# Relaid pools, spread block ends and projection columns in a five-stage graph network kernel

## The chip, the cores and the metric

The kernel runs on one core of one Trainium2 chip. The metric is device time in microseconds (us), lower is better. The profiles are hardware profiles of single executions. All executions here are of the fast state as far as one core can tell, save one of the kernel before (3599.67 us, left out of its round's ratios). They still scatter by up to ±30 us; what goes with that is shown near the end.

## The reference, cut to what matters

2708 nodes with 512 features, a dense 0/1 adjacency matrix (about 2.4% ones), and four residual layers, each followed by a layer norm:

```python
# layer 0: mean over the first 64 neighbours of each row
keep = Ab & (cumsum(Ab, axis=1) <= 64)
xj = leaky_relu((keep @ X / max(cnt, 1)) @ W_nb.T + b_nb)
x = layernorm(x + leaky_relu(X @ W_line.T + b_line) + where(cnt > 0, xj, 0))
# layer 1: mean over all neighbours
nb = (mask @ x / deg) @ W_nb + b_nb
x = layernorm(x + relu(concat([x @ W_self + b_self, nb]) @ W_comb + b_comb))
# layers 2 and 3: graph attention with 8 heads of 64; s = Wh @ a1, d = Wh @ a2
e = leaky_relu(s[:, :, None] + d[:, None, :], 0.2)
h = softmax(where(adj > 0, e, -9e15)) @ Wh
# layer 3 goes on: elu, one more attention with a single head of 512 ("last"),
# elu, relu(@ lin1) @ lin2; then x = layernorm(x + h)
```

The kernel folds `W_self @ W_comb[:512]` and `W_nb @ W_comb[512:]` into one weight each. In what follows a "tile" is 128 nodes, so 22 tiles, the last of 20 rows.

## The kernel before

Layer 0's first stage makes `y = x @ W_nb.T` and the `W_line` term for each tile, and turns each row block of the adjacency matrix into a transposed mask. After it comes the folding of layer 1's weights, then layer 0's aggregation in blocks of four tiles:

```python
for t in range(NT):                                   # mask projection
    xt = fetched(sm, x, t, n, "xt")                   # two buffers
    xT = transposed(sm, ps_tr, xt, n, "xT")           # TensorE, copied out by ScalarE
    # pm = xT @ wnT -> keep_y ; pm = xT @ wlT -> u    (8 float32 matmuls)
    nc.gpsimd.tensor_add(u[:n], u[:n], xt)
    nc.scalar.dma_start(r0_dram[...], u[:n])
    mask(t)                                           # 22 transposes into PSUM
# ... here the weights of layer 1 are folded, TensorE, 58 us ...
for b0 in range(0, NT, 4):                            # aggregation
    kT = kept(0)                                      # cum on TensorE, compare on VectorE
    for j in range(NT):
        if j + 1 < NT:
            nxt = kept(j + 1)
        # pa[t] += kT.T @ yH[j], yL[j]  for the four tiles of the block
        kT = nxt
    for t in ts_:                                     # the block's end, all at once
        # bias, leaky, residual, layer norm on VectorE, store x1
```

The projections of layers 2, 3 and last (`project`) take s and d on VectorE and write v for all tiles at the end:

```python
for t in range(NT):
    xT = transposed(sm, ps_tr, source(sm, t, n), n, "xT")   # three row buffers
    # pm = xT @ w
    for i, col in enumerate((scol, dcol)):
        pr = sm.tile([P, D], F32, name="pr")
        nc.vector.tensor_mul(pr[:n], pm[:n], ab[:n, i, :])
        nc.vector.tensor_reduce(col[:n, t, :heads], pr..., AX.X, OP.add)
    # ecol, ucol = exp(d) ; R2 = pm * ecol ; vrow = exp(clipped s), transposed
nc.sync.dma_start(v_dram, vrow)          # attention reads it back, broadcast
# bcol and the parts (bfloat16 splits of ucol * ecol and ecol) for all tiles
```

Every stage opens its own pools for SBUF and PSUM, and each waits for the memory of one before it.

Of the kernel before, what the change touches and what calls it, by code (L numbers as in the profile page):

```python
# [29 lines left out]
def kernel(  # L30
# [34 lines left out]

    upper = const.tile([P, P], BF16, name="upper")
    make_upper_triangular(nc, upper)
    below = const.tile([P, P], BF16, name="below")
    nc.vector.tensor_scalar(below, upper, -1.0, 1.0, op0=OP.mult, op1=OP.add)
# [13 lines left out]
    scol = const.tile([P, NT, H], F32, name="scol")  # L83
    dcol = const.tile([P, NT, H], F32, name="dcol")
    for c in (scol, dcol):
        nc.vector.memset(c, 0.0)
# [6 lines left out]
    x1_dram = dram.tile([N, D], F32, name="x1_dram")  # L93
    z1_dram = dram.tile([N, D], F32, name="z1_dram")
# [23 lines left out]
    def transpose_weight(pool, psum, dst, src, queue):  # L118

        for ki in range(KD):  # L120
            wr = pool.tile([P, D], F32, name="wr", bufs=3)
            queue.dma_start(wr, src[ki * P:(ki + 1) * P, :])
            ps = psum.tile([P, KD, P], F32, name="ps_tr")
            for ko in range(KD):
                nc.tensor.transpose(ps[:, ko, :], wr[:, ko * P:(ko + 1) * P], ident)
            nc.vector.tensor_copy(dst[:, :, ki * P:(ki + 1) * P], ps)

    def fetched(pool, src, t, n, name, bufs=None):
        x_ = pool.tile([P, D], F32, name=name, bufs=bufs)
        nc.sync.dma_start(x_[:n], src[t * P:t * P + n, :])  # L130
        return x_[:n]

# [6 lines left out]

    with ExitStack() as phase:  # L140
        yp = phase.enter_context(tc.tile_pool(name="y", bufs=1))
        yH = yp.tile([P, NT, D], F32R, name="yH")
# [3 lines left out]
        b_nb = yp.tile([P, D], F32, name="b_nb")  # L146
        nc.scalar.dma_start(b_nb, bcast(l0_b_nb, D))
# [4 lines left out]

        with ExitStack() as ph:
            wp = ph.enter_context(tc.tile_pool(name="l0w", bufs=1))
            sm = ph.enter_context(tc.tile_pool(name="l0s", bufs=2))
            ps_tr = ph.enter_context(tc.tile_pool(name="ps_tr", bufs=2, space=PSUM))
            ps_mm = ph.enter_context(tc.tile_pool(name="ps_mm", bufs=2, space=PSUM))
            ps_tb = ph.enter_context(tc.tile_pool(name="ps_tb", bufs=2, space=PSUM))
            b_line = wp.tile([P, D], F32, name="b_line")
            nc.scalar.dma_start(b_line, bcast(l0_b_line, D))  # L160
            wnT = wp.tile([P, KD, D], F32, name="wnT")
            wlT = wp.tile([P, KD, D], F32, name="wlT")
            transpose_weight(sm, ps_tr, wnT, l0_w_nb, nc.sync)
            transpose_weight(sm, ps_tr, wlT, l0_w_line, nc.scalar)

            def mask(t):
                n = rows(t)
                m = sm.tile([P, N], BF16, name="m")
# [12 lines left out]
                for g0 in range(0, NT, G):  # L181
                    g1 = min(g0 + G, NT)
                    ps = ps_tb.tile([P, G, P], BF16, name="ps_tb")
# [8 lines left out]

            for t in range(NT):
                n = rows(t)
                xt = fetched(sm, x, t, n, "xt")
                xT = transposed(sm, ps_tr, xt, n, "xT")
                pm = ps_mm.tile([P, D], F32, name="pm")
                for k in range(KD):
                    nc.tensor.matmul(pm[:n], xT[:, k, :n], wnT[:, k, :], start=(k == 0), stop=(k == KD - 1))
                keep_y(t, n, pm)  # L200
                pm = ps_mm.tile([P, D], F32, name="pm")
                for k in range(KD):
                    nc.tensor.matmul(pm[:n], xT[:, k, :n], wlT[:, k, :], start=(k == 0), stop=(k == KD - 1))
# [4 lines left out]
                nc.scalar.dma_start(r0_dram[t * P:t * P + n, :], u[:n])  # L208
                mask(t)



        wp = phase.enter_context(tc.tile_pool(name="l1wp", bufs=1))
        wself = wp.tile([P, KD, D], F32, name="wself")
        wnb = wp.tile([P, KD, D], F32, name="wnb")
        bias1 = wp.tile([P, D], F32, name="bias1")
        with ExitStack() as ph:
            lw = ph.enter_context(tc.tile_pool(name="l1w", bufs=1))
            ps_tr = ph.enter_context(tc.tile_pool(name="ps_trw", bufs=2, space=PSUM))
            ps_mm = ph.enter_context(tc.tile_pool(name="ps_mmw", bufs=2, space=PSUM))  # L220
            ps_b = ph.enter_context(tc.tile_pool(name="ps_bw", bufs=1, space=PSUM))
            bcomb = lw.tile([P, D], F32, name="bcomb")
            nc.scalar.dma_start(bcomb, bcast(l1_b_comb, D))
            pb = ps_b.tile([P, D], F32, name="pb")
            for i, (w_in, b_in, dst) in enumerate(((l1_w_self, l1_b_self, wself), (l1_w_nb, l1_b_nb, wnb))):
                wT = lw.tile([P, KD, D], F32, name="wT")
                transpose_weight(lw, ps_tr, wT, w_in, nc.sync)
                wc = lw.tile([P, KD, D], F32, name="wc")
                nc.scalar.dma_start(wc, l1_w_comb[i * D:(i + 1) * D, :].rearrange("(k p) c -> p k c", p=P))
                bcol = lw.tile([P, KD], F32, name="bcol", bufs=2)  # L230
                with nc.allow_non_contiguous_dma(reason="512 numbers, once"):
                    nc.scalar.dma_start(bcol, b_in.rearrange("(k p) -> p k", p=P))
                for m in range(KD):
                    pm = ps_mm.tile([P, D], F32, name="pm")
                    for k in range(KD):
                        nc.tensor.matmul(pm, wT[:, k, m * P:(m + 1) * P], wc[:, k, :],  # L236
                                         start=(k == 0), stop=(k == KD - 1))
                    nc.scalar.copy(dst[:, m, :], pm)
                brep = lw.tile([P, KD, P], F32, name="brep")
                nc.vector.tensor_copy(brep, bcol[:, :, None].to_broadcast([P, KD, P]))  # L240
                for k in range(KD):
                    nc.tensor.matmul(pb, brep[:, k, :], wc[:, k, :],
                                     start=(i == 0 and k == 0), stop=(i == 1 and k == KD - 1))
            nc.vector.tensor_add(bias1, pb, bcomb)



        with ExitStack() as ph:
            sm = ph.enter_context(tc.tile_pool(name="l0b", bufs=2))
            ps_a = ph.enter_context(tc.tile_pool(name="ps_a0", bufs=1, space=PSUM))  # L250
            ps_c = ph.enter_context(tc.tile_pool(name="ps_c0", bufs=2, space=PSUM))
            for b0 in range(0, NT, 4):
                b1 = min(b0 + 4, NT)
                ts_ = range(b0, b1)
                cols, w = slice(b0 * P, b1 * P), (b1 - b0) * P
                r0 = {t: fetched(sm, r0_dram, t, rows(t), f"r0{t - b0}", 1) for t in ts_}
                cum = ps_c.tile([P, 512], F32, name="cum")
                pa = {t: ps_a.tile([P, D], F32, name=f"pa{t - b0}") for t in ts_}

                def kept(j):  # L260
                    nc.tensor.matmul(cum[:, :w], upper, maskT[:, j, cols], start=(j == 0), stop=True,  # L261
                                     skip_group_check=True)
                    kT = sm.tile([P, 512], F32R, name="kT", bufs=3)
                    nc.vector.scalar_tensor_tensor(kT[:, :w], cum[:, :w], KEEP, maskT[:, j, cols],  # L264
                                                   op0=OP.is_le, op1=OP.mult)
                    return kT

                kT = kept(0)
                for j in range(NT):
                    if j + 1 < NT:  # L270
                        nc.tensor.matmul(cum[:, :w], below, maskT[:, j, cols], start=False, stop=True,
                                         skip_group_check=True)
                        nxt = kept(j + 1)
                    for t in ts_:
                        for y in (yH, yL):
                            nc.tensor.matmul(pa[t], kT[:, (t - b0) * P:(t - b0 + 1) * P], y[:, j, :],  # L276
                                             start=(j == 0 and y is yH), stop=(j == NT - 1 and y is yL))
                    kT = nxt
                us = {}
                for t in ts_:  # L280
                    n = rows(t)
                    us[t] = sm.tile([P, D], F32, name=f"u{t - b0}", bufs=1)
                    nc.vector.scalar_tensor_tensor(us[t][:n], pa[t][:n], rkeep[:n, t:t + 1], b_nb[:n],
                                                   op0=OP.mult, op1=OP.add)
                for t in ts_:
                    n, u = rows(t), us[t]
                    leaky(u[:n], u[:n])
                    nc.vector.scalar_tensor_tensor(u[:n], u[:n], has[:n, t:t + 1], r0[t], op0=OP.mult, op1=OP.add)
# [698 lines left out]
```

## Time and profile before

| | before |
|---|---|
| median, the three runs known when the prediction was made | 3582.98 us (3557.87 to 3584.34) |
| span of the profiled run | 3581.7 us |
| TensorE (PE) busy | 3330.2 us, 93% |
| mean granted clock of TensorE | 0.944 |

Names of tiles that the profile lines use: kT is a kept mask, pa (before) or acc (after) the sums of layers 0 and 1, pm the product of a tile of rows with a weight (in the changed kernel's aggregation also the running count of neighbours, cum before), xT those rows transposed, po and pn the sums of the head attentions and of the last one, e the masked attention weights before the softmax's division. A wait row reads: engine, tile and line that waited, what ended the wait, then us in total, times, longest.

Only TensorE is close to full. The prediction below shows the lines that say so: its busy tenths over 40 slices, the busy time by stage, and its waits. In a row of busy time by stage the columns are the stretch and its length, then the busy us (and number of instructions) of PE, PEld (weight loads), DVE (VectorE), ACT (ScalarE) and POOL (GpSimd), then the granted clock of TensorE, the DMA share and GB/s.

### The profile page before, as it was taken

To read this page: it belongs to the slowest core of one execution; us is meant where nothing else is said; L and a number is where in the kernel's file an instruction comes from. 1 tells how busy PE (TensorE), PEld (TensorE's weight loads), DVE (VectorE), ACT (ScalarE), POOL (GpSimd) and SP (SyncE) were. 2 spreads that over 40 slices of the span, in tenths; PEclk is the share of its full clock that TensorE was granted. 3 is DMA by queue.
4 is the path that set the end of the run, shared out by engine and by line. 5 is a ranking of instruction groups with operands and counts; after the bars stand their busy time and mean duration, and the time that the engine had idled before them with its cause. 6 is when DMAs were issued, how large, how long until landed. Compare 5 with 4: busy or idle time off the path is not lost.

```text
span 3581.7 us, 39258 instructions
## 1 busy us (share of the span) xinstructions
PE 3330.2 (93%) x15914; PEld 1695.5 (47%) x15914; DVE 2001.2 (56%) x2526; ACT 1380.9 (39%) x1519; POOL 158.3 (4%) x188
## 2 busy tenths in 40 slices
PE   7989898899988999999977999999988999999998
PEld 4445565447863444443432444443443545454546
DVE  5542445212337888999868988989783222122122
ACT  2420000112222877888823878878740101010000
POOL 1210000000000000000021000000000000000000
PEclk9999899999999999999988999999899999999999
DMA  5540101212221000000052000000021000000000
GB/s 119 124 111 27 47 24 39 65 59 76 79 80 61 17 30 28 24 23 23 16 151 86 25 25 25 24 23 31 19 77 65 15 12 27 1 24 0 24 7 19
DMA packets 103809, 157.14 MB, mean 44 GB/s; under 512 B 22442, under 2 KB 44234, under 8 KB 103602
## 3 DMA queue, kind: packets, MB, share of 16 engines
q1 hardware_dynamic: 72236, 102.17, 9.2%
q10 hardware_dynamic: 25590, 37.71, 3.0%
q0 software_dynamic: 5792, 14.67, 2.5%
q8 instruction: 127, 2.08, 0.2%
q14 instruction: 64, 0.52, 0.0%
HBM read 124.62 MB, written 44.55 MB: 47 GB/s over the span
## 4 chain that ended last, share of the span: by engine, by line
PE 84%; DVE 6%; DMA 5%; issue 3%; POOL 1%; ACT 1%; SPq 0%; POOLq 0%; ACTq 0%; DVEq 0%
PE po L506 26%; PE pn L659 14%; PE pd L492 7%; PE pa L323 6%; PE pa L276 6%; PE pm L396 5%; PE pl L625 5%; PE pl L635 4%; PE pm L302 2%; PE pm L306 2%; DMA m<-in_adj_dram 2%; PE ps_t L524 1%; DMA o<-o_dram 1%; DVE m L171 1%; PE pm L236 1%
## 5 line engine op out<-in xcount | busy, mean ns | idle before, releaser
L453 DVE SCALAR_TENSOR_TENSOR e<-v_bc,ucol,maskT 128x1408 f32<-128x1408 f32 (+5 forms) x836 | 1191.1, 1477 | 447.6 <-PE pn L659 370.9
L461 ACT ACTIVATE c<-e,bcol 128x1300 bf16<-128x1300 f32 (+1 forms) x704 | 998.7, 1424 | 217.2 <-DVE e L453 174.8
L506 PE MATMUL po<-e,R 128*64 128x512 f32 (+4 forms) x4224 | 960.1, 566 | 14.7 <-issue 14.4
L506 PEld LDWEIGHTS po<-e,R 128*64 128x64 f32 (+1 forms) x4224 | 364.0, 140 | 515.5 <-issue 439.0
L659 PE MATMUL pn<-e,R 128*128 128x512 f32 (+3 forms) x1056 | 425.2, 544 | 8.2 <-DVE e L453 8.2
L659 PEld LDWEIGHTS pn<-e,R 128*128 128x128 f32 (+1 forms) x1056 | 190.9, 190 | 219.7 <-issue 219.5
L570 ACT ACTIVATE elu_e<-elu_e 128x512 f32<-128x512 f32 (+2 forms) x46 | 27.5, 603 | 632.5 <-DVE elu_e L569 631.8
L396 PE MATMUL pm<-w,xT 128*128 128x512 f32 (+1 forms) x528 | 247.6, 613 | 19.3 <-ACT xT L115 12.2
L115 ACT COPY xT<-ps_tr 128x512 f32<-128x512 f32 x110 | 60.1, 568 | 449.8 <-DMA x<-x_dram 344.5
L492 PE MATMUL pd<-c,parts_c 128*6 128x512 bf16 (+4 forms) x2112 | 221.4, 360 | 0.0
L492 PE MATMUL pd<-maskT,parts_m 128*6 128x512 fp8e4 (+2 forms) x2112 | 210.8, 361 | 9.8 <-DVE parts_m L371 9.8
L276 PE MATMUL pa<-yH,kT 128*128 128x512 f32 x484 | 216.7, 448 | 0.0
L625 PE MATMUL pl<-lin 128*128 128x256 f32 (+1 forms) x704 | 163.7, 394 | 38.2 <-DVE lin L572 38.2
L276 PE MATMUL pa<-yL,kT 128*128 128x512 f32 x484 | 193.9, 401 | 0.0
L323 PE MATMUL pa<-yH,mf 128*128 128x512 f32 x484 | 189.4, 391 | 3.6 <-ACT mf L320 3.6
L323 PE MATMUL pa<-yL,mf 128*128 128x512 f32 x484 | 189.2, 391 | 0.0
L264 DVE SCALAR_TENSOR_TENSOR kT<-cum,maskT 128x512 fp32r<-128x512 f32 (+1 forms) x132 | 84.8, 646 | 164.5 <-PE cum L261 164.5
L625 PEld LDWEIGHTS pl<-lin 128*128 128x128 f32 x704 | 137.5, 204 | 72.4 <-DVE lin L572 49.8
L396 PEld LDWEIGHTS pm<-w,xT 128*128 128x128 f32 (+1 forms) x528 | 94.9, 191 | 134.8 <-issue 102.0
L635 PE MATMUL pl<-lin,gT 128*128 128x512 f32 (+1 forms) x352 | 153.0, 592 | 0.0
L638 DVE TENSOR_TENSOR y<-pl,x 128x512 f32<-128x512 f32 (+1 forms) x22 | 15.2, 691 | 244.3 <-PE pl L635 244.3
L659 PE MATMUL pn<-e,ecol 128*128 128x512 f32 (+2 forms) x264 | 125.9, 559 | 0.0
(162 smaller groups left out, 2906.2 us busy)
## 6 DMA issues: line engine op xcount, KB each, us to landing
x<-x_dram SPq DMA_DIRECT2D x105, 256.0 KB
m<-in_adj_dram POOLq DMA_DIRECT2D x21, 677.0 KB, 6.7
v_bc<-v_dram SPq DMA_DIRECT2D x16, 704.0 KB
x_dram<-u ACTq DMA_DIRECT2D x42, 256.0 KB
o<-o_dram SPq DMA_DIRECT2D x42, 256.0 KB
v_bc<-v_dram SPq DMA_DIRECT2D x16, 650.0 KB
o_dram<-o SPq DMA_DIRECT2D x32, 256.0 KB
xt<-in_x_dram SPq DMA_DIRECT2D x21, 256.0 KB
```

The lines of the kernel that those rows point to most:

```text
L264: nc.vector.scalar_tensor_tensor(kT[:, :w], cum[:, :w], KEEP, maskT[:, j, cols], op0=OP.is_le, op1=OP.mult)
L276: nc.tensor.matmul(pa[t], kT[:, (t - b0) * P:(t - b0 + 1) * P], y[:, j, :], start=(j == 0 and y is yH), stop=(j == NT - 1 and y is yL))
L302: nc.tensor.matmul(pm[:n], xT[:, k, :n], wnb[:, k, :], start=(k == 0), stop=(k == KD - 1))
L323: nc.tensor.matmul(pa, mf[:, j - g0, :], y[:, j, :], start=(j == 0 and y is yH), stop=(j == NT - 1 and y is yL))
L396: nc.tensor.matmul(pm[:n], xT[:, k, :n], w[:, k, :], start=(k == 0), stop=(k == KD - 1))
L453: nc.vector.scalar_tensor_tensor(e[:n, :w], v[:n, :w], ucol[:n, j, h:h + 1], maskT[:n, j, c0:c0 + w], op0=OP.max, op1=OP.mult)
L461: nc.scalar.activation(c[:n, :w], e[:n, :w], AF.Sigmoid, bias=bcol[:n, j, h:h + 1], scale=STEP)
L492: nc.tensor.matmul(pd[i][g:g + 6, :c1 - c0], lhsT, rhs, start=(j < 2 and what == 0), stop=(j >= NT - 2 and what == 1))
L506: nc.tensor.matmul(po[i][HO * k:HO * k + HO, :c1 - c0], R2[:n, j, h * HO:(h + 1) * HO], e[:n, c0:c1], start=(j == 0), stop=(j == NT - 1))
L625: nc.tensor.matmul(pl[:, :w], self.lin1[:, k, f * P:(f + 1) * P], h[:, k, :w], start=(k == 0), stop=(k == KD - 1))
L635: nc.tensor.matmul(pl[:n], gT[:, f, (t - t0) * P:(t - t0) * P + n], self.lin2[:, f, :], start=(f == 0), stop=(f == KF - 1))
L659: nc.tensor.matmul(pn[:, k, :w], lhsT, e[:n, :w], start=(j == 0), stop=(j == NT - 1))
```

## The change

Its intent is to remove TensorE's pauses at stage borders and block ends, by five means:

1. The fold of layer 1's weights stands first; its result goes to memory and is loaded back later.
2. Layer 0's block ends are a generator (`finish`), stepped once per step of the next block; the next block's first kT is made in the last step of this one.
3. Rows of all stages share one pool of two buffers (`ahead`), weights another, so that loads can go out before a stage begins. Several stores move to SyncE's queue.
4. `wa` = weights times the attention vectors, summed per head, is made once during the mask projection (24 loads, products and sums); s and d then come from four narrow matmuls per tile (`psd`).
5. v, the parts and bcol are written per block of tiles rather than after the last tile.

```diff
+    with ExitStack() as ph:                      # part 1: the fold, first
+        ... nc.scalar.dma_start(w_dram[i][m * P:(m + 1) * P, :], wm)
@@ mask projection
+            def vectors():                       # part 4
+                for layer, (w_src, w_view, a_srcs, heads) in enumerate(atts):
+                    for i in range(2):
+                        ab = st.tile([P, D], F32, name="ab", bufs=1)
+                        nc.scalar.dma_start(ab.rearrange(...), a_srcs[i])
+                        for k in range(KD):
+                            wr = st.tile([P, D], F32, name="wr")
+                            nc.scalar.dma_start(*w_view(wr, w_src, k))
+                            nc.vector.tensor_mul(wr, wr, ab)
+                            nc.vector.tensor_reduce(wa[:, layer, k, i, :heads], ..., AX.X, OP.add)
+                            yield
-                xt = fetched(sm, x, t, n, "xt")
+                xt = fetched(x, t, n)            # part 3: the shared pool
...
+                if t >= 5:
+                    for _ in range(2):
+                        next(todo, None)
@@ aggregation
+                    elif i + 1 < len(cuts):      # part 2
+                        cum, nxt = begin(cuts[i + 1])
...
+                    next(todo, None)             # one step of the last block's end
...
+                todo = finish(ts_, us)
@@ project
+                psd = ps_v.tile([P, 2, H], F32, name="psd")
+                for k in range(KD):              # part 4
+                    nc.tensor.matmul(psd[:n, :, :heads], xT[:, k, :n], wa[:, layer, k, :, :heads], ...)
-                for i, col in enumerate((scol, dcol)):
-                    ... tensor_mul, tensor_reduce
...
+                if t == z - 1:                   # part 5: last tile of a block
+                    nc.sync.dma_start(v_dram[:, cols], vrow[:, ...])
+                    ... parts of this block
```

## The prediction

> **What bounds the kernel now.** I read the page first, then the busy time by stage, then PE's waits, then the order of time around each stage border. The page: PE is busy 93% of 3581.7 us, and the chain that ended last runs on it.
>
> ```profile
> PE 84%; DVE 6%; DMA 5%; issue 3%; POOL 1%; ACT 1%; SPq 0%; POOLq 0%; ACTq 0%; DVEq 0%
> PE   7989898899988999999977999999988999999998
> PEclk9999899999999999999988999999899999999999
> ```
>
> So only two things can save time: less work for PE, or fewer of its 251.5 us of idleness (3581.7 - 3330.2) together with the slow clock that follows each pause. The eights and sevens of the second and third line mark the stage borders. The windows by stage say where the idleness lies (columns: stretch, its us, then PE, PEld, DVE, ACT and POOL busy, the granted clock, the DMA share, GB/s):
>
> ```profile
> 0.00:246.00 246.00, 213.31 (x956) 110.31 (x956) 136.63 (x303) 82.76 (x133) 50.17 (x56) 0.98 0.53 116
> 246.00:304.50 58.50, 44.91 (x112) 21.66 (x113) 6.21 (x10) 4.68 (x8) 0.00 (x0) 0.80 0.25 77
> 304.50:634.00 329.50, 287.16 (x1227) 201.88 (x1225) 150.70 (x275) 0.00 (x0) 13.19 (x20) 0.93 0.10 33
> 1044.00:1153.50 109.50, 92.64 (x290) 43.81 (x294) 75.61 (x147) 26.24 (x110) 0.00 (x0) 0.94 0.22 62
> 1818.00:1946.00 128.00, 99.00 (x286) 42.32 (x286) 100.23 (x223) 26.35 (x109) 32.86 (x36) 0.93 0.39 114
> ```
>
> These are, in order: layer 0's projection with the mask; the folding of layer 1's weights; layer 0's aggregation; the projections of layers 2 and 3. The two head attentions (664.5 and 654 us, PE busy 97 and 98%) and the last one (875.7 us) keep their inner loops, so I leave them as they are. What PE waited for, all stages, its costliest rows (us in total, times, longest):
>
> ```profile
> PE cum L271 <- DVE kT L264: 41.2, 7, 8.8
> PE pl L625 <- DVE lin L572: 38.2, 6, 7.2
> PE ps_tr L113 <- DMA x<-x_dram: 22.2, 2, 11.6
> PE po L506 <- issue: 14.4, 2, 7.3
> PE ps_v L415 <- DVE b L411: 12.7, 8, 3.0
> ```
>
> The first row is layer 0's block ends: DVE finishes four tiles there while PE waits for the next kept mask. The second row (the last layer's block ends) is not touched by the change. The third and fourth are borders: a stage's first rows arrive late, and attention waits for the whole v to go to memory and back.
>
> A pause costs more than itself. In order of time, at a block end of layer 0 and a few us later:
>
> ```profile
> 366.69 0.58 PE L271 MATMUL cum<-maskT,below 128*128 128x512 fp8e4 x1 [7.81 <-DVE kT L264]
> 368.35 0.63 PE L276 MATMUL pa<-yH,kT 128*128 128x512 f32 x1
> ...
> 373.03 0.39 PE L276 MATMUL pa<-yH,kT 128*128 128x512 f32 x1
> ```
>
> After the 7.81 us wait the same matmul takes 0.63 instead of 0.39 us, and matmuls start 0.43 instead of 0.23 us apart, for some 4.5 us: about 2 us more are lost.
>
> **What the Trainium skill says.** "TensorE: Matmul & The Clock Gate", Part 1: PE falls to half its clock after about 3.4 us of idleness, and needs about 3.4 us of work to return. This trace agrees (0.43 against 0.23 us, for 4.5 us). The same page, "LDWEIGHTS": a load takes its columns divided by 1.2 GHz, 107 ns for 128. The trace agrees as a rate: eight loads in 0.97 us, one of them 0.19 long, so 0.11 us apart:
>
> ```profile
> 1797.28 0.97 PEld L524 LDWEIGHTS ps_t<-pick,dT 102*128 102x128 f32 x8
> ```
>
> "DMA: Bandwidth & Descriptors", "Why small descriptors are slow", gives 27% overhead at 256 bytes; here the head weights come in 256-byte pieces, and beside them the first x of layer 2 landed after 5.7 us (issued 1044.78, PE at 1050.5), against 2.9 at layer 1's start (642.34 to 645.2). "TensorE: Matmul & The Clock Gate", the table at its head: the other engines are strict FIFO, so a DVE or ACT instruction that waits holds all behind it; the 7.81 us above agree.
>
> **The change part by part.** The scheduler places instructions by readiness (the loads of layer 3's rows stand ahead of the last stores of layer 2 in the trace, 1797 against 1803), so I assume that loads with a free buffer really go ahead.
>
> 1. *Fold first, then the projection.* Now the first product is at 25.6 us, the projection runs to 246, the fold to 304.5, the first pa at 306.9. The 64 + 16 fold matmuls at 0.43 are 34.4 us; with transposes, 12 us for the first 1 MB and the cold start I take 58. Then eight transposed weight tiles at 0.75 us: 6. All rows and the first two masks are there by then. The projection now takes 22 tiles in 221 us, 10.0 each, of which PE needs 16 x 0.43 + 22 mask transposes at 0.06 + 0.66, about 9. The chain there is a loop of POOL's add, 5.3 us of issue, 6.7 of mask DMA, 3.0 of DVE's count and 2.4 more of DVE, for two tiles. Four PSUM buffers for the mask help a little. Against it, the vectors for the s and d columns put 24 x (0.68 + 0.68) = 33 us on DVE, 6 MB on the DMA rings and up to 1 us per issue on ACT, over twelve tiles; some hides in DVE's idle 109 us of 246. I take 10.2 per tile, 225. Sum 58 + 6 + 225 = 289: **-17**. This is my weakest term (-40 to +5).
> 2. *Layer 0's block ends spread.* A steady step is 2.30 us, in the last block 1.16: 22 x (5 x 2.30 + 1.16) = 278.5, against 329.5: 51 to gain. The spread work is 3.8 us of DVE per tile, 76 in all, beside 0.69 per step for kT. The step with the norm (0.74 + 0.68 + 0.17 + 0.15 + about 1.0 for POOL's power + 0.55) exceeds the 1.6 us free in a step, with about one step of slack. I take back 0.45 us for each of 20 such steps: **-42**.
> 3. *Borders.* Layer 0 to 1: 11.6 idle plus 2.3 cold; the last two tiles' own chain and a row load stay: -6. Layer 1's second half, mf ready earlier: -3. To layer 2: 10.7 idle (w's issue holds the SP queue 4.8 us) plus 1.1 cold: -10. Layer 2's attention to 3, and 3's to 4, where w comes after the first transposes: -8 and -8. Together **-35**.
> 4. *s and d as columns.* DVE loses two products and two sums per tile, 4 x 0.68 less about 0.15. But PE gains four f32 products of 16 columns, each two instructions as now (528 for 66 tiles of 4), each paced by its weight load: 8 x 0.11 = 0.86 us per tile. The projections of layers 2 and 4 are PE-bound (8.52 and 8.46 us for two tiles, of which 6.88 are pm), so 22 x 0.86 = 19, less about 1 for shorter waits: **+18** each. Layer 3 is DVE-bound (100 of 128 us; about 5.5 per tile); it becomes PE at 5.1 or the loop of two row buffers (load 2.6, add 1.3, norm 2.5, store 2.3, halved: 4.4): **-7**.
> 5. *v per block.* Layer 2 to its attention: 2.5 + 4.9 + 7.3 idle and 2 cold = 16.7; what stays is the last eviction and clearing pd, about 3: **-14**. Layer 3 the same: **-14**. Last layer: 2.6 + 0.5 + 8.2 + 2.3 cold = 13.6, less 2.5: **-11**.
>
> Sum: -17 - 42 - 35 + 18 + 18 - 7 - 14 - 14 - 11 = -104, from 3583 to **3479 us**, -2.9%.
>
> **The rivals.** (a) *Hidden columns.* The narrow products could slip under other PE work, or the scheduler could fill PE's pauses with them: the 36 us of part 4 vanish, 3440 us. For it: PEld is 47% busy and overlaps PE. Against it: weight loads as the pace at 1797. (b) *DVE becomes layer 0's bound*, by the norms between the kept masks and by the vectors in the projection: parts 1 and 2 give 25 together instead of 59, 3515 us. For it: FIFO, one kT of lookahead. Against it: DVE is busy only 46% of the aggregation. (c) *Loads don't go ahead.* Stores now share the SP queue, and each pool still waits for the memory of one before it; if borders keep half their waits, some 35 us are lost: 3514. (d) *Two row buffers instead of three* make layer 3's projection DMA-latency-bound, at 6.3 per tile: +18, 3497.
>
> **Range and chances.** Parts 2, 3 and 5 are removals of measured idleness; part 1 can err by 20, part 4 by 18 each way, and the baseline itself ran from 3557.87 to 3584.34. One or two rivals together reach 3535; (a) with a full gain in parts 1 and 2 reaches 3415. Faster by over 2% means under 3511: I give 0.77; within 2% 0.21; slower 0.02.
>
> **What would show it.** Right: the cum wait on kT falls from 41 to under 10 us; the aggregation takes about 288 us; the projections of layers 2 and 4 go to some 10.2 us for two tiles with psd at about 0.86 per tile; po and pn no longer wait 7 to 8 us at their start; PE's total idleness falls by 110 to 140 us. Wrong: the mask projection stretching over 240 us behind m, wr or ACT; new waits of ps_tr on rows in layer 3; psd taking 0.3 us or 2 us a tile; kT late by more than 0.5 us at each norm.

## The result

| | before | after |
|---|---|---|
| median | 3583.66 us (3557.87 to 3592.75, 4 runs) | 3540.97 us (3531.24 to 3549.69, 4 runs) |
| span of the profiled run | 3581.7 us | 3547.8 us |
| TensorE busy | 3330.2 us | 3375.2 us |
| mean granted clock | 0.944 | 0.957 |

The ratio of after to before is 0.9891 (95% interval 0.9842 to 0.9939). All ratios here are the mean time of one kernel's fast runs over that of the other's of the same rounds, so they are not quite the ratio of the medians. The change is a gain of 1.1%, inside the 2% that counts as the same, and the time lies above the predicted range.

From the page of the changed kernel, TensorE's busy tenths and granted clock over 40 slices, and the chain that ended last by engine:

```profile
PE   7789998999999999999988999999999999999998
...
PEclk9999999999999999999889999999999999999999
...
PE 83%; DVE 4%; issue 3%; DMA 1%; POOL 1%; ACT 1%; ACTq 0%; POOLq 0%; SPq 0%; DVEq 0%
```

Most of the sevens and eights inside the row have gone; they stay at the start (77, 8), in slice 7, which ends in the border into layer 1, in slices 21 and 22, layer 3's projection, and in the last slice. Busy time by stage in the changed kernel, in the order start and fold, mask projection, aggregation, projections of layer 2 and layer 3:

```profile
0.00:82.30 82.30, 57.32 (x239) 32.75 (x239) 30.29 (x85) 14.71 (x23) 10.25 (x17) 0.90 0.56 157
82.30:328.50 246.20, 206.70 (x838) 102.49 (x835) 139.67 (x278) 71.36 (x119) 39.09 (x38) 0.94 0.56 127
328.50:616.00 287.50, 280.55 (x1222) 195.49 (x1222) 145.33 (x271) 12.57 (x21) 15.60 (x21) 1.00 0.12 42
1023.50:1138.30 114.80, 109.65 (x447) 60.69 (x448) 33.01 (x97) 40.78 (x120) 6.38 (x22) 0.98 0.18 60
1790.20:1921.70 131.50, 117.58 (x447) 63.40 (x448) 62.96 (x177) 37.76 (x119) 47.82 (x62) 0.93 0.41 126
```

Three stages stand out against the prediction's rows: the aggregation is full (280.55 of 287.50 at clock 1.00), the mask projection is not (206.70 of 246.20 at 0.94), and layer 3's projection has lost a third of VectorE's work (62.96 for 100.23) without getting shorter. TensorE's waits in the changed kernel:

```profile
PE pl L675 <- DVE lin L622: 38.2, 6, 7.2
PE ps_tr L107 <- DMA rows<-in_x_dram: 21.7, 12, 3.4
PE psd L450 <- ACT xT L109: 17.4, 31, 5.3
PE ps_tr L107 <- DVE ln_rs L99: 14.5, 2, 11.6
...
PE pm L341 <- DVE kT L313: 5.6, 9, 1.3
```

The 41.2 us for kT have become 5.6. New are the rows of x in the mask projection (21.7; none in that stage before). The border into layer 3 waits 11.6 us in one piece, where before it waited 5.8 and 4.5. Marks between the stages (first or last matmul of each) give the whole account, in us, from the two profiled runs:

| stretch | before | after | difference | predicted |
|---|---|---|---|---|
| start to the first aggregation matmul | 306.9 | 328.5 | +21.6 | -17 |
| layer 0's aggregation | 326.8 | 287.5 | -39.3 | -42 |
| border into layer 1 | 13.4 | 8.1 | -5.3 | -6 |
| layer 1 | 392.8 | 391.5 | -1.3 | -3 |
| border into layer 2 | 12.4 | 7.9 | -4.5 | -10 |
| projection 2, to attention's first matmul | 109.7 | 114.8 | +5.1 | +4 (18 - 14) |
| attention 2 | 642.4 | 636.1 | -6.3 | 0 |
| border into layer 3 | 14.4 | 15.8 | +1.4 | -8 |
| projection 3 | 132.6 | 131.5 | -1.1 | -21 (-7 - 14) |
| attention 3 | 645.0 | 634.7 | -10.3 | 0 |
| border into the last attention's projection | 11.2 | 5.5 | -5.7 | -8 |
| projection 4 | 105.6 | 117.1 | +11.5 | +7 (18 - 11) |
| last attention to the end | 868.4 | 868.8 | +0.4 | 0 |
| sum (with rounding) | 3581.7 | 3547.8 | -33.9 | -104 |

So 70 us are missing, or 87 without the 16.6 us that the two head attentions gained and that no part had forecast. 38.6 are in the first row, 29 in layer 3's projection and the border before it.

### The profile page after: what moved, and what is told of

The parts are those of the page before. It is cut to its first block, busy times and chain, and to the rows that moved or that the text cites. A ratio compares the mean times of both kernels' runs of the same rounds, so it can differ in the third digit from the quotient of the medians.

```text
span 3547.8 us, 40357 instructions
## 1 busy us (share of the span) xinstructions
PE 3375.2 (95%) x16442; PEld 1752.5 (49%) x16442; DVE 1878.1 (53%) x2397; ACT 1406.4 (40%) x1555; POOL 176.4 (5%) x232
## 4 chain that ended last, share of the span: by engine, by line
PE 83%; DVE 4%; issue 3%; DMA 1%; POOL 1%; ACT 1%; ACTq 0%; POOLq 0%; SPq 0%; DVEq 0%
PE po L568 26%; PE pn L707 14%; PE pd L554 7%; PE acc L384 6%; PE acc L348 5%; PE pm L454 5%; PE pm L228 5%; PE pl L675 5%; PE pl L685 4%; PE ps_t L586 2%; PE psd L450 1%; PE ps_t L600 1%; POOL ln_rs L100 1%; PE pm L341 1%; ACT xT L109 1%
## 5 line engine op out<-in xcount | busy, mean ns | idle before, releaser
L568 PE MATMUL po<-e,R 128*64 128x512 f32 (+4 forms) x4224 | 945.6, 560 | 2.7 <-DVE R L462 2.7
L454 PE MATMUL pm<-w,xT 128*128 128x512 f32 (+1 forms) x528 | 254.0, 626 | 0.0
L348 PE MATMUL acc<-yH,kT 128*128 128x512 f32 x484 | 213.4, 441 | 0.1
L384 PE MATMUL acc<-yL,mf 128*128 128x512 f32 x484 | 193.0, 399 | 0.0
L348 PE MATMUL acc<-yL,kT 128*128 128x512 f32 x484 | 191.2, 395 | 0.0
L384 PE MATMUL acc<-yH,mf 128*128 128x512 f32 x484 | 190.7, 394 | 0.0
L228 PE MATMUL pm<-w,xT 128*128 128x512 f32 (+1 forms) x352 | 173.1, 637 | 15.7 <-ACT xT L109 10.9
L228 PE MATMUL pm<-weight,xT 128*128 128x512 f32 (+1 forms) x352 | 158.3, 592 | 0.5 <-DVE u L287 0.5
L313 DVE SCALAR_TENSOR_TENSOR kT<-pm,maskT 128x512 fp32r<-128x512 f32 (+1 forms) x132 | 84.9, 644 | 127.5 <-PE pm L311 127.2
```

The source lines that it names most:

```text
L228: nc.tensor.matmul(pm[:n], xT[:, k, :n], w[:, k, :], start=(k == 0), stop=(k == KD - 1))
L313: nc.vector.scalar_tensor_tensor(kT[:, :w], cum[:, :w], KEEP, maskT[:, j, cols], op0=OP.is_le, op1=OP.mult)
L348: nc.tensor.matmul(pa[t], kT[:, (t - b[0]) * P:(t - b[0] + 1) * P], y[:, j, :], start=(j == 0 and y is yH), stop=(j == NT - 1 and y is yL))
L384: nc.tensor.matmul(pa, mf[:, j - g0, :], y[:, j, :], start=(j == 0 and y is yH), stop=(j == NT - 1 and y is yL))
L454: nc.tensor.matmul(pm[:n], xT[:, k, :n], w[:, k, :], start=(k == 0), stop=(k == KD - 1))
L568: nc.tensor.matmul(po[i][HO * k:HO * k + HO, :c1 - c0], R2[:n, j, h * HO:(h + 1) * HO], e[:n, c0:c1], start=(j == 0), stop=(j == NT - 1))
```

## The experiments

Each is the changed kernel with an edit; all gave correct results. Since whole times scatter, the verdicts rest on the stretches of the profiled runs, one profile each, and the times are given beside them. How well a stretch repeats is seen in the kernels whose edit does not touch it: start to the first aggregation matmul 323.1 to 328.5 us in seven kernels, the aggregation 287.1 to 288.8 in all but e7 (with vectors inside it too), projection 2 114.4 to 115.0 in nine, layer 3's projection 129.9 to 133.0 in seven. The kernel before had a median of 3581.1 to 3583.8 us in these rounds. Fifteen kernels were run.

### Why the mask projection grew

**e1_vec_agg** moves the making of `wa` out of the mask projection:

```diff
@@ mask projection
-                if t >= 5:
-                    for _ in range(2):
-                        next(todo, None)
@@ aggregation, in the loop over j; ab and wr in tiles that lie free there
                     next(todo, None)
+                    if j % 5 == 4:
+                        next(vecs, None)
```

> The changed kernel with one part moved: the 24 loads, products and sums that make wa (the extra weight columns) leave layer 0's mask projection and are done inside layer 0's aggregation, in two tiles of the pool that lie free there. Theory A (this work disturbs the mask projection: ScalarE's queue waits for VectorE's sums before it copies xT and yH on, and its loads take DMA time): the stretch from the start to the first pa, 328.5 us in the changed kernel, falls to about 305 (22 tiles at 10.0 us as in the kernel before), the aggregation stays within 287 to 293, and the whole falls by some 15 to 23 us, to about 3520. Rival B (the loss is the ring of two row buffers, which is freed by an add that GpSimd only reaches after the next mask's load): still above 320, the whole changes by under 8 us.

Measured: 3516.37 us median, ratio 0.9862 (0.9773 to 0.995, so unclear at 2%). The first aggregation matmul comes at 300.2 instead of 328.5 us, and the aggregation stays at 287.9. In the changed kernel ScalarE's waits in the mask projection include these, which do not appear among those of e1:

```profile
ACT xT L109 <- DVE wa L275: 29.3, 4, 9.5
...
ACT yH L222 <- DVE wa L275: 13.0, 2, 8.7
```

The busy time by stage of e1, mask projection and aggregation:

```profile
80.20:300.20 220.00, 196.31 (x837) 96.69 (x837) 109.55 (x229) 71.01 (x118) 38.98 (x38) 0.99 0.47 108
300.20:588.10 287.90, 280.68 (x1223) 196.18 (x1222) 174.99 (x320) 12.57 (x21) 15.21 (x21) 1.00 0.23 68
```

The mask projection is back at 10.0 us per tile, its clock at 0.99, and VectorE's 30 us of vectors lie beside the aggregation at no cost (174.99 against 145.33 busy, same length). TensorE's wait for xT in this stage falls from 10.5 to 0.3 us, and for the rows of x from 21.7 to 13.4. Theory A holds in that the vectors are the cause. How they act is read from the waits: a load of `wr` on ScalarE's queue waits for VectorE's sum to free its buffer, and the copies of xT and yH stand behind it in order. The edit moved the loads, their bytes and VectorE's work together; no run moved one of them alone.

**e2_vec_rows3** adds a third row buffer:

```diff
-                xt = fetched(x, t, n)
+                xt = fetched(x, t, n) if t % 3 < 2 else fetched(x, t, n, st, "row3", 1)
```

> As e1_vec_agg, and the rows of x in the mask projection have three buffers in place of two (the third in the space that the vectors left). Theory A: no more than 3 us better than e1_vec_agg. Rival B (rows freed late): start to first pa 8 to 20 us shorter than in e1_vec_agg, near 300, and PE's waits for the rows of x (21.7 us in the changed kernel's whole trace) under 5 us.

Measured: the first aggregation matmul at 301.9 us, against 300.2 in e1. Rival B falls, as far as it is tested with the vectors gone: TensorE's wait for rows of x goes from 13.4 us to none, but the waits for yL, u and m grow (4.9 to 9.6, 3.3 to 5.6 and 0.7 to 8.2) and the stretch is no shorter. The whole run was at 3502.09 us median (ratio 0.98, 0.9723 to 0.9876, unclear), but the 12 us by which its profile is shorter than that of e1 are all in attention 3 (622.2 for 634.6), which the edit does not touch.

**e10_bc_first** swaps two issues at the very start, since the order of time in the changed kernel shows VectorE waiting for 2 KB of bias columns with the copies of the first transposed weight behind it:

```profile
10.54 0.43 DVE L188 COPY brep<-bc 128x512 f32<-128x512 f32 x1 [8.09 <-DMA bc<-in_L_gnn_b_self_dram]
...
22.51 0.43 DVE L188 COPY brep<-bc 128x512 f32<-128x512 f32 x1 [11.55 <-DMA bc<-in_L_gnn_b_nb_dram]
...
24.56 3.78 PE L182 MATMUL pm<-wc,wT 128*128 128x512 f32 x4 [6.86 <-DVE wT L120]
```

```diff
-            load_weight(wc, l1_w_comb[i * D:(i + 1) * D, :], nc.scalar)
             bc = lw.tile([P, KD], F32, name="bc")
             ... nc.scalar.dma_start(bc, b_in.rearrange("(k p) -> p k", p=P))
+            load_weight(wc, l1_w_comb[i * D:(i + 1) * D, :], nc.scalar)
```

> The changed kernel with two issues swapped at its start: the loads of the bias columns (2 KB in 512 pieces) stand before those of the comb weights (1 MB) on ScalarE's queue. Theory H (the fold's start is held by VectorE waiting 11.6 us for the second bias column, with the copies of wT behind it): the first product of the fold (24.6 us in the changed kernel) comes at 17 to 20, the first pm of layer 0 (82.3) at 75 to 78. Rival (the start is bound by the bytes of its loads): both within 2 us.

Measured: the fold's first product at 19.0 us instead of 24.6, the first pm of layer 0 at 74.8 instead of 82.3; 3542.05 us, ratio 0.9868. Theory H holds, but this pair flatters it. In the twelve kernels with the old order the two marks lie at 24.0 to 25.0 and 79.2 to 83.2 us (mean 80.8); in the four with the new order (e10, e12, e14, e15) at 19.0 to 20.8 and 74.8 to 79.0 (mean 76.5). So the swap gains about 5 us at the first product and about 4 at the first pm.

**e14_line_act** further puts the line weights' four loads on ScalarE's queue (`transpose_weight(st, ps_tr, wlT, l0_w_line, nc.scalar)`).

> As e10_bc_first, and the four loads of layer 0's line weights on ScalarE's queue as in the kernel before, not behind the others on SyncE's. Theory I (at the end of the fold TensorE waits for these loads, since both weights share one queue and two buffers): the first pm of layer 0, 74.8 us in e10_bc_first, comes at 68 to 71. Rival (the two buffers or the bytes of the adjacency's loads set it, not the queue): 74 to 76.

Measured: first pm at 76.4 us; a miss. The queue alone is not what holds these loads; TensorE still waits 4.8 us for them (5.0 in e10). Whether it is the two buffers or the bytes was not tried. The mask projection after it was 236 instead of 246 us; I have no reason for that. The time was 3528.3 us, ratio 0.9857.

### Whether the spread block ends are the aggregation's gain

**e7_no_ends** undoes part 2 alone (with it, the sums are read out by VectorE again, as in the kernel before, and not by ScalarE):

```diff
-                todo = finish(ts_, us)
+                for _ in finish(ts_, us):
+                    pass
-                    elif i + 1 < len(cuts):
-                        cum, nxt = begin(cuts[i + 1])
@@ at the head of each block
+                cum, kT = begin(b)
```

> The changed kernel with part 2 undone: at the end of each block of layer 0 its four tiles are finished at once on VectorE, and the next block's first kT is made after that. Theory (the spreading is what shortened the aggregation): the aggregation, first pa to last, goes from 287 back to 322 to 328 us, and no other stage changes by over 3 us; the whole about 3576. Rival (the shorter aggregation comes from the early load of the weights and rows, or from the clock): under 300.

Measured: the aggregation at 328.2 us, with the clock down to 0.94 and TensorE's wait for kT back, and the median at 3581.54 us over 20 runs, ratio 1.0004 (0.9981 to 1.0027). In words: without part 2 the whole change is worth nothing. Busy time of that stretch, then the wait:

```profile
327.60:655.80 328.20, 289.59 (x1222) 201.48 (x1222) 149.05 (x272) 0.00 (x0) 12.29 (x21) 0.94 0.11 37
```

```profile
PE pm L339 <- DVE kT L313: 38.8, 7, 8.4
```

### Layer 3's projection

In the changed kernel the marks of psd show that up to tile 9 (counted from 0) two tiles take some 10.5 us, and that the eight tiles from 9 to 17 take 57.2 us where 42 would be right. In that stretch, work of the attention appears: v of the first block has been written, so four of its `e` (VectorE, 1.68 us each) and four of its sigmoids run early. ScalarE then changes tables between exponential and sigmoid. The order of time:

```profile
1863.35 1.28 ACT L522 ACT_TABLE_LOAD   x1
1866.13 1.28 ACT L459 ACT_TABLE_LOAD   x1
1868.00 1.28 ACT L522 ACT_TABLE_LOAD   x1
```

The duration agrees with the Trainium skill, "ScalarE activation tables: per-element evaluation and per-set limits", section "What a function is on this engine", which puts two functions of different sets one load of 1283 ns apart.

**e3_bcol_end** keeps the sigmoids out:

```diff
-                    nc.gpsimd.tensor_scalar(bcol[:n, t, :], ucol[:n, t, :], ...)
@@ after the last tile
+            if heads > 1:
+                nc.vector.tensor_scalar(bcol, ucol, -STEP * (1.0 + 2.0 ** -22), None, op0=OP.mult)
```

> The changed kernel, but bcol (the bias of the sigmoid) is made for all tiles in one instruction after the last tile, as in the kernel before, so that no sigmoid of the attention can run inside the projection; v and the parts stay per block. Theory C (attention work that the early v lets into the projection holds it up: the sigmoids put table loads of 1.28 us between ScalarE's exponentials, and xT waits behind them): table loads of ScalarE fall from 19 to about 7, layer 3's projection (first pm to first po) falls from 131.5 to about 118 to 122 us with the two border waits growing by 2 to 5 us each, the whole by 5 to 12 us. Rival D (the chain of row loads, two buffers deep, sets layer 3's projection): it stays at 129 to 133 and the whole within 3 us.

Measured: table loads 19 to 9, but the projection only from 131.5 to 128.0 us, and 3550.12 us over 14 runs (ratio 0.9921), no gain. Theory C as I put it falls: the tables are visible and cost at most 3.5 us here (128.0 lies 1.9 us under the range in which the stage repeats).

**e8_v_once** undoes part 5 (`a, z = 0, NT` for the blocks, and bcol after the last tile as in e3):

> The changed kernel with part 5 undone: v, the parts and bcol are written once after the last tile. If the early v is worth what the prediction took (14, 14 and 11 us): projection 2 goes from 114.8 to about 128, layer 3's from 131.5 to 140 to 145, or less if the parts and early attention work in the middle of it cost what they seem to (then about 132), projection 4 from 117 to about 128. Rival (it was hidden anyway): each within 3 us of the changed kernel.

Measured, in us: projection 2 from 114.8 to 122.8, projection 4 from 117.1 to 121.5, and layer 3's from 131.5 *down* to 123.3; 3552.81 us, ratio 0.9942. So the early v gains 8.0 and 4.4 us, and loses 8.2 in layer 3. A stretch of about equal length from the middle of layer 3's projection (from 48 us after its start in the changed kernel, from 54 in e8), in the changed kernel and then in e8:

```profile
1838.00:1896.00 58.00, 48.12 (x177) 26.39 (x175) 31.20 (x77) 23.33 (x52) 22.41 (x26) 0.88 0.47 153
```

```profile
1840.00:1896.00 56.00, 54.24 (x229) 30.05 (x228) 23.94 (x75) 11.89 (x54) 18.18 (x20) 1.00 0.37 119
```

With v once, TensorE is full (54.24 of 56) at clock 1.00; with v per block, VectorE has 7 us more work there (parts and e), and TensorE waits often enough to lose its clock (0.88).

**e4_x2_late** gives the second operand of layer 3's rows a pool that was opened before attention 2, and **e5_rows_late3** gives the first operand three buffers there as well. In the changed kernel the load of x2 waits for attention's last store, 1.77 us after the latter was issued (order of time, SyncE's queue and GpSimd's add):

```profile
1776.58 0.35 SPq L614 DMA_DIRECT2D o_dram<-o  x1
1778.35 5.84 SPq L134 DMA_DIRECT2D x<-x_dram  x4
1781.35 2.48 POOL L630 TENSOR_TENSOR rows<-rows,x 128x512 f32<-128x512 f32 x2 [646.89 <-DMA x<-x_dram]
```

```diff
+    late = till.enter_context(tc.tile_pool(name="late", bufs=2))
-    o, x2 = fetched(o_dram[0], t, n), fetched(x2_dram, t, n, sm, "x2")
+    o, x2 = fetched(o_dram[0], t, n), fetched(x2_dram, t, n, late, "x2")          # e4
+    o, x2 = fetched(o_dram[0], t, n, late, "o", 3), fetched(x2_dram, t, n, late, "x2")   # e5
```

> The changed kernel, but the second operand of layer 3's rows (x2) lies in a pool of its own, two deep, opened before layer 2's attention, so that it can be loaded ahead over the border, which the change did for the first operand alone. Theory E (the border into layer 3 did not shrink since x2's memory came free only with the attention's last store): from the last product of attention 2 to the first pm of layer 3, 22.9 us falls to 12 to 15 us; the projection itself stays at 128 to 132; the whole falls by 8 to 11. Rival F (the border is bound by the normalisation's chain, not by the load): it stays above 20.

> As e4_x2_late, and the first operand of layer 3's rows has three buffers of its own in place of the two that it shares with every other stage. Theory D (in layer 3 a row buffer is held by load, add, normalisation and store before the next load may start, so two of them set the pace): layer 3's projection, first pm to first po, falls from 131 to about 118 to 122 us, and no chain piece of the kind 'store of x, then load of o' is left in it. Rival G (the hold-up in the middle, some 20 us between tiles 10 and 17, is VectorE's: the first block's parts and the attention's first products stand in its queue ahead of the normalisation): it stays above 127 us, with the same gaps after the first block's end.

Measured: e4 shortens the border from 15.8 to 10.5 us (my 22.9 in the expectation counted it from an earlier mark, the last product; the shift, 5.3 us, is less than the 8 I expected) and leaves the projection at 130.9; 3538.32 us, ratio 0.9885. In e5 the projection takes 125.6 us: 58 us for its first half with TensorE 56.5 busy, but 67 for the rest with 58.9. So both theories have a part: the third buffer gains 5 us, and rival G's gap after the first block's end stays. The time was 3532.08 us, ratio 0.9858. The border into layer 2 shrank too, from 7.9 to 3.2 us, which I had not foreseen.

**e6_sd_dve** undoes part 4 in all three projections (products and sums on VectorE again, no psd, no `wa`):

> The changed kernel with part 4 undone: s and d of every tile come from two products and two sums on VectorE as in the kernel before, there is no psd on TensorE, and the vectors (wa) and their work in the mask projection are gone. If part 4 costs what the traces suggest: start to first pa 300 to 306 (from 328.5), projection 2 about 97 to 102 (from 114.8), projection 4 about 94 to 100 (from 117.0), layer 3's projection 128 to 140 (from 131.5, since VectorE is then nearly full), in all some 50 to 60 us less than the changed kernel, about 3485. Rival (the vectors cost nothing, psd lies beside other work): within 15 us of the changed kernel.

Measured: start to first aggregation matmul 301.7, projection 2 102.1, projection 4 101.2, the last two 0.1 and 1.2 us above what was expected, but layer 3's projection 176.0. The whole stayed at 3544.72 us, ratio 0.9904: 55 us gained in three stages, 44 lost in one, and 14 lost in the attentions, of which more below. Busy time of that stage, and a few lines of its chain in order of time (start, us, what), one round of two tiles, 16.8 us:

```profile
1754.40:1930.30 175.90, 120.26 (x279) 52.45 (x279) 104.16 (x233) 38.79 (x118) 44.92 (x62) 0.81 0.32 102
```

```profile
1803.48 2.62 DMA rows<-o_dram
...
1806.26 1.28 POOL rows L612
...
1808.47 1.17 DVE pr L437 x2
...
1820.28 2.57 DMA rows<-o_dram
```

No engine is full: VectorE 59%, TensorE 68% at clock 0.81. It is a loop of load, add, normalisation behind the last tile's products, transposes, product, and the load again when a row buffer is free.

**e13_sd_rows3** is e6 with three buffers for layer 3's first operand (and `pr` and x2 with one, to make room).

> e6_sd_dve (s and d on VectorE in all three projections) with three buffers for the first operand of layer 3's rows in place of two, and one of its own for the second. Theory D (with two row buffers layer 3's projection runs at the latency of load, add, normalisation, and VectorE's products in between, 16.5 us per two tiles in e6_sd_dve): it falls from 176 to 130 to 145 us. Rival G (VectorE's queue alone sets it): it stays above 165. The other stages as in e6_sd_dve.

Measured: 135.6 us instead of 176.0; 3499.48 us, ratio 0.9759. Theory D holds here: the two shared row buffers cost 40 us of this stage when s and d are on VectorE, and psd hid most of that.

### Putting it together

**e9_mixed** keeps part 4 in layer 3 alone, and makes its eight sets of vectors inside the aggregation.

> The changed kernel with part 4 kept for layer 3 alone: layers 2 and the last take s and d on VectorE again, layer 3 from psd, and the eight sets of vectors left are made inside layer 0's aggregation. If the costs found stage by stage add up: start to first pa about 301, projection 2 about 102, layer 3's 130 to 133 (not the 176 of e6_sd_dve), projection 4 about 101, the whole 50 to 60 us under the changed kernel, about 3487. Rival (layer 3's 176 us came from the vectors' removal from elsewhere, not from VectorE's s and d in it): layer 3's projection stays over 150.

Measured: projection 2 103.5, layer 3's 132.6, projection 4 103.8, first aggregation matmul at 307.6 (6 us later than expected, not explained); 3494.45 us, ratio 0.9746 (0.9694 to 0.9798). That is 46.5 us under the changed kernel, a little less than the 50 to 60 expected.

**e11_v3_x2** takes v once in layer 3 only, with x2 ahead:

```diff
-                a, z = next(c for c in cuts if c[0] <= t < c[1])
+                a, z = next(c for c in cuts if c[0] <= t < c[1]) if layer != 1 else (0, NT)
```

> The changed kernel with part 5 undone in layer 3 alone (v, parts and bcol once after its last tile), and x2 loaded ahead as in e4_x2_late. Layer 3's projection 120 to 124 us as in e8_v_once, the border before it 5 us shorter as in e4_x2_late, projections 2 and 4 as in the changed kernel (115 and 117): the whole 10 to 16 us under the changed kernel. If the early v of layer 3 pays elsewhere, attention 3 is longer by what is gained.

Measured: border 10.5, projection 127.7 (not 120 to 124), 3544.81 us, ratio 0.9898: no gain over the changed kernel in the whole time. Border and projection together take 138.2 us, against 139.6 in e8 and 147.3 in the changed kernel: what is loaded ahead is partly waited for later.

**e12_best2** and **e15_best3** combine the favoured edits; they differ in layer 3's v (once in e12, per block in e15) and in the line weights' queue.

> All that the runs favour together: e9_mixed, layer 3's v once, x2 ahead, three row buffers in the mask projection, and the bias columns loaded first. Sums of the stages: start to first pa 296 to 302, aggregation 288, projection 2 102, layer 3's 121 to 124 with a border of 17, projection 4 101; the whole 65 to 80 us under the changed kernel, about 3470, a ratio to the kernel before of about 0.97.

> As e12_best2, but layer 3's v per block as in the change, and the line weights on ScalarE's queue. If layer 3's early v is worth nothing in this setting as in the changed kernel, its projection is 131 us in place of 127 with the attention after it unchanged, and the whole is within 8 us of e12_best2; if x2 loaded ahead was what it lacked, 122 to 125 and some 3 to 5 us faster.

Measured: e12 3485.14 us, ratio 0.9728 (0.968 to 0.9775); e15 3474.83 us, ratio 0.9704 (0.9675 to 0.9733). Both beat both kernels; e12 falls some 15 us short of what the sums promised. Layer 3's projection takes 127.1 in e12 and 133.4 in e15, so its early v loses 6 us here too (3 between e4 and e11, 130.9 and 127.7); e15's lead in time lies in its attentions (631.2 and 623.4 us against 637.0 and 638.8), which have the same code in both kernels.

## Why the prediction was wrong, point by point

Three steps failed: the start and the vectors of part 1 (38.6 us worse than predicted), the early v of layer 3 in part 5 (22.2) and the border into layer 3 in part 3 (9.4). Together they are the 70 us; the smaller misses elsewhere and the attentions' unforeseen gain nearly cancel.

**Part 1 (-17 predicted, +21.6 measured) is the largest failure**, and the prediction called it its weakest term (its sum of 289 us against 306.9 is -18 when rounded). Two steps failed. The vectors were put down as partly hidden in VectorE's idle time, 10.2 us per tile against 10.0; they cost 26 us (246.2 against 220.0 us in e1), by the waits through ScalarE's order rather than VectorE's load. The prediction had named the right mechanism, strict order, and not applied it to ScalarE's loads. And the 64 us from the start to the first product were 82.3. The fold's last product came at 62.5 us for the 58 allotted; the step to the first product after it took 19.8 for 6. The eight transposed weight tiles took 5.7 us of TensorE there, as predicted, but 7.5 us of the first tiles' mask transposes lie among them, which the prediction counted later, and TensorE waits 6.0 us for the line weights. The bias columns account for about 4 of the 82 us (e10 and the three kernels like it); the queue does not account for the line weights (e14), and what does stays open. The four PSUM buffers brought nothing that shows: e1's 10.0 us per tile is before's. What was right is the order itself: without the vectors the first aggregation matmul comes 6.7 us earlier than before (300.2 against 306.9).

**Part 2 (-42, measured -39.3)** was right in mechanism and size; undone, it returns 40.7 us (e7). Rival (b) is split. Its first half, VectorE's norms between the kept masks, did not happen: kT's wait is 5.6 us in total. Its second half did, the vectors in the projection, though by the waits in ScalarE's order: parts 1 and 2 gave 18 us together where rival (b) said 25 and the prediction 59.

**Part 3 (-35, measured -15.4 over the five stretches)** was right in kind and too large. The border into layer 3 failed outright (+1.4 for -8): the second operand's pool lay in memory that attention still held, so its load could not go ahead. This is rival (c); e4 took 5.3 us of it away, and 10.5 stay; what sets them was not tried. The border into layer 2 gave 4.5 of 10; in e5 and e13, where layer 3's first operand left the shared pool, it fell by another 4.7, and why is not shown.

**Part 4 (+18, +18, -7).** psd takes 0.96 to 1.07 us for its eight instructions in most tiles, from the first start to the last end, where 0.86 was predicted; the starts are 0.10 to 0.11 us apart, as predicted, and rival (a) did not happen. Undoing it (e6) gives 12.7 and 15.9 us back in layers 2 and 4, a little under the 18. For layer 3 the size came out, -9.3 for -7: with v once the stage takes 123.3 us (e8) against 132.6 before, at 10.3 us for two tiles with TensorE busy 111.45 us, which is the 5.1 us per tile on TensorE that the prediction named. What hides it in the changed kernel is part 5. The premise "DVE-bound (100 of 128 us)" was wrong: VectorE was not full before, and with s and d on VectorE the stage takes 176 us with two row buffers, bound by no engine, and 136 with three (e6, e13). Rival (d) had named the two buffers, at +18; with psd the third buffer and x2's pool together are worth 6 us, without it 40.

**Part 5 (-14, -14, -11)** gave -8.0, +8.2 and -4.4 us (e8). The step that failed is "Layer 3 the same", +8.2 us for -14: the removed wait was real, but early v lets the attention's first `e` and the block's parts into VectorE's queue ahead of layer 3's norms, in a stage that has norms on its chain. Layer 2's projection has none. That it is VectorE's queue rather than ScalarE's tables rests on e3 against e8 (128.0 and 123.3 us); the parts and the `e` were not tried apart.

**Not predicted:** 16.6 us in the two head attentions; as far as the runs tell, this is luck, without which the miss would have been larger. The 17 profiles here have 34 such attentions with nearly the same instructions, and they take 616.8 to 650.9 us, in step with the granted clock: 616.8 to 623.5 at 0.98 to 0.99, 642.4 to 650.9 at 0.94 to 0.95. Before's two (642.4 at 0.95 and 645.0 at 0.94) and after's (636.1 at 0.95, 634.7 at 0.96) lie inside that scatter, before's near its upper end, so no part of the change is needed to explain them; that the change has no effect there is not shown, since before has one profile.

## What to carry to other kernels

Work that is "off the critical engine" still has to be placed in some engine's order: put it where that engine's queue holds nothing that the critical one waits for, which here turned 26 us into nothing. Before data are made available early, ask which later stage becomes ready by it, and what it will stand in front of. Few buffers shared by all stages are sized for the easiest stage; here the stage with a norm between load and product needed one more, and its loss showed as low busy shares everywhere (e6).

## What the Trainium skill lacked or had wrong

- "TensorE: Matmul & The Clock Gate", Part 1, ties the half clock to an idle window (its section on a second failure mode adds micro-idles between groups). In these traces TensorE dropped to half its clock at the end of some pairs of heads while it was busy throughout, and at others not; what triggers it stays open. Busy time of the changed kernel at one such end, and at the next:

```profile
1208.00:1212.00 4.00, 4.00 (x27) 0.48 (x24) 3.78 (x3) 3.17 (x5) 0.00 (x0) 0.54 0.30 120
1212.00:1216.00 4.00, 4.00 (x14) 2.06 (x13) 1.09 (x1) 3.51 (x4) 0.00 (x0) 0.50 0.00 0
1216.00:1220.00 4.00, 4.00 (x21) 3.98 (x23) 0.18 (x1) 1.05 (x1) 0.00 (x0) 0.50 0.00 0
```

```profile
1298.00:1302.00 4.00, 4.00 (x32) 3.05 (x33) 1.21 (x2) 3.65 (x3) 0.00 (x0) 1.00 0.00 0
```

  The matmul ends are modelled, so short gaps could hide in the 4.00. In the traces' record of the granted clock, 191 of the 204 stretches at half clock in the 34 attentions begin within 8 us of the end of a pair of heads. Inside one attention they sum to 14.5 to 81.5 us, and half of that difference is 33.5 us. Across the profiles one attention varies by 34 us in step with its clock, and whole runs of one kernel do so as well (the kernel before: 3544.1 us at a mean clock of 0.955, 3590.7 at 0.940).
- "DMA: Bandwidth & Descriptors", "Why small descriptors are slow", gives its overhead at 256 bytes and no time for a load in 4-byte pieces. A load of 512 separate numbers (2 KB) was still waited for 14.6 us after its issue at the busy start (issued at 1.8 us, used at 16.4 in e10).
- No page has what a load costs that stands in an engine's order ahead of that engine's own work: 26 us here for 24 of them on ScalarE (with their sums on VectorE and their bytes, which no run separates).
